# Two short segments' depthwise convolution on TensorE, and the scan's x multiplied from PSUM, in a Mamba-2 and gated-FFN kernel

## The chip, the cores and the metric

The kernel runs on one core of one Trainium2 chip. The metric is the device time of one launch in microseconds. The core has five engines that run side by side and wait for one another through semaphores: TensorE (PE, matrix products, into PSUM), VectorE (DVE), ScalarE (ACT), GpSimd (POOL, which works on SBUF alone here) and SyncE (SP, which issues most transfers). PSUM has eight banks of 512 fp32 columns here.

## The reference

The input is u of 4 batches x 1024 tokens x 256 features. One layer of two halves follows, each with a residual and layernorms (`_layernorm` without weights), all in fp32:

```
x = x + LN(mamba2(LN(x)))          # 4 x 1024 tokens, 256 features
x = x + LN(ffn(LN(x)))

mamba2(u):
  z, xBC, dt = split(u @ in_proj)            # 512, 768, 8 columns
  xBC = silu(b + sum_k w[:, k] * xBC[t - 3 + k])   # depthwise, causal, 4 taps
  x, B, C = split(xBC)                       # 512 (8 heads x 64), 128, 128
  dt = softplus(dt + dt_bias); dA = -exp(A_log) * dt
  y_t = C_t . S_t,  S_t = exp(dA_t) S_{t-1} + B_t (dt_t x_t);  y += D * x
  y = rmsnorm(y * silu(z)) * norm_weight;  return y @ out_proj

ffn(x): gate, up: 256 -> 2048 with 4-bit weights and a scale per 32; gelu(gate) * up;
        down: 2048 -> 256 with 4-bit weights and scales
```

## The kernel before

**Segments.** `SEGS` (line 25) cuts the 4096 tokens into nine segments: the first 512 tokens of batch 0 as two short segments, 0 and 1, of 256 tokens each, then seven of 512. A segment first goes through `mixer(s)` (line 646, the Mamba half) and then through `ffn(s)` (line 962). Features lie on partitions: the 768 columns of xBC are six tiles of 128 (`NF`), with tokens along the free axis.

**The mixer.** `norm_in` normalises and turns tokens around to `xnT`. `step_sizes` makes dt and dA, `decays` their running sums and exponentials. `features(f)` (line 753) multiplies one tile of in_proj by `xnT` into a PSUM bank `pp`, and forms the convolution: ScalarE writes `h`, tile f of `xc`, as `pp * w3 + b`; VectorE then adds the three earlier taps, one instruction each, from shifted views of `pp`. Weights and bias are halved once in `prepare_small` (line 558), so that `(tanh(h) + 1) * h` is the silu: ScalarE makes the tanh into `th`, VectorE the product. The last three columns of `pp` are saved in `tails[b]` for the next segment of the batch; `carried` (line 736) has GpSimd work out, from the tails of the segment before, the share of the first three columns (`edge`), which VectorE adds.

`inner(i)` (line 776) works on one block of 128 tokens: the decays between tokens (`e`), then four transposes of `xc` into a bank `px`, which ScalarE copies to `xt` (line 813), and from which VectorE makes `xdt` = x dt and `xw` = x dt decay (lines 816 and 819); GpSimd makes `y` = x D; two more products give C.B and B turned around. `gate(c)` makes silu(z), `scan(i)` the three products of the scan, `gated`, `way_out` and `turned` the gating, the output projection, the residual, and the turned input of the second half, `xfT`.

**The second half.** For segments 0 and 1 `widen(n)` makes gate and up of 128 hidden units in one bank (16 times), `narrow` the down product. Later segments use a scheme of seven products for eight blocks (`seven`), for which `weight_sums` forms sums of the weights on GpSimd in the tile `sums` and stores them by transfers (`stock`). `unpack` (line 585) turns 4-bit weights into fp32 in the opening: VectorE on the codes, GpSimd on the products with the scales (`wide`, `wd`).

**The order of work.** Nothing is issued as it is written. `Recorder` takes down every operation with its buffers; `issue` (line 260) then plans: at each step it takes, for each engine, the operations that could start soonest by its own table of costs (`weigh`, line 227) and picks by `rank`. Buffers come from pools and are assigned in that plan. The result is one fixed order per engine, and each engine runs its queue strictly in that order, so every instruction has line 347 in the profile and is told by its tiles. For VectorE instructions without a PSUM operand the plan adds up to `PORT` ns while GpSimd is at work, as long as the planned time is below `EARLY` (lines 33 and 311). The waiting room within which rank may prefer a later operation is 150 ns before `EARLY` and 30 ns after it (line 1135). Forty `WARM` products of the identity with itself (lines 1099 to 1104) have the last rank and fill TensorE in the opening.

**PSUM.** Two banks `a` serve the mixers, four `f` the gate and up products, two `d` the down products. The mixer of segment 0 takes its banks from `f`, that of segment 1 alternately from `d` and `a` (`ps_a`, line 654).

Of the kernel before, what the change touches and what calls it, by code (L numbers as in the profile page):

```python
# [24 lines left out]
SEGS = [(0, 0, 256), (0, 256, 256)] + [(b, 0, 512) for b in range(1, NB)] + \  # L25
    [(b, 512, 512) for b in range(NB)]
TMAX = 512
# [2 lines left out]
PORT = 700.0  # L30
SWITCH = 1400.0
WARM, WARM_FROM = 40, 9000.0
EARLY = 60000.0
FRONT = 2 + 1 + NF
MASKED = -1.0e30
MLP = 2048
# [337 lines left out]
def mamba_ffn_kernel(  # L374
# [19 lines left out]
    r = Recorder(tc.nc)  # L394
# [11 lines left out]
    def given(ap):  # L406
# [10 lines left out]
    pools = {  # L417
        "x": pool("x", [P, CMAX, DM], 3), "xnT": pool("xnT", [P, 2, TMAX]),
        "xc": pool("xc", [P, NF, TMAX]), "xn": pool("xn", [P, DM], 2, 3), "th": pool("th", [P, TMAX], 3, 3),
        "sz": pool("sz", [P, DI // P, TMAX]), "r": pool("r", [P, DI // P, P], 2), "e": pool("e", [P, NH, P], 2), "xt": pool("xt", [P, DI], 2),  # L420
        "bt": pool("bt", [P, DS], 2), "xdt": pool("xdt", [P, NH, HD], 2),
        "xw": pool("xw", [P, NH, HD], 2), "y": pool("y", [P, DI // P, P], 3),
        "yo": pool("yo", [P, DI // P, P]), "xf": pool("xf", [P, 2, P], 2),
        "xfT": pool("xfT", [P, 2, TMAX], 2), "act": pool("act", [P, HALF], 3, 3),
        "fo": pool("fo", [P, DM], 2), "cst": pool("cst", [CMAX * NH, P], 2),
        "rows": pool("rows", [CMAX * NH, P], 2, of=hbm), "dec": pool("dec", [P, 3 * CMAX * NH], 2),
        "edge": pool("edge", [P, NF, 3], 2), "part": pool("part", [P, NF, 3], 2),
        **{k + who: pool(k + who, shape, 4, 4) for who in "mf"
           for k, shape in (("mv", [P, CMAX, 2]), ("st", [P, 6]), ("rs", [P, CMAX]))},
        "one": pool("one", [P, 1], 24, 8),  # L430
# [4 lines left out]
    def get(tag):  # L435
        return pools[tag].get()
# [96 lines left out]
    def over_heads(v, n):  # L533

        return v.unsqueeze(2).to_broadcast([P, NH, n])
# [19 lines left out]
        return mv  # L555


    def prepare_small():

        r.scalar.activation(aneg, aneg, AF.Exp)  # L560
        r.vector.tensor_scalar_mul(aneg, aneg, -1.0)
        r.floor = 7500.0
        r.vector.tensor_scalar_mul(cw, cw, 0.5)
        r.vector.tensor_scalar_mul(cb, cb, 0.5)
        r.floor = 0.0

    def prepare_z():
# [76 lines left out]
    xfT = {}  # L644

    def mixer(s):
# [88 lines left out]

        def carried():
            v_["xc"] = by_segment(s, "xc", lambda t, c: t[:, :, c])
            if t0 == 0:
                return

            tail = tails[b]
            edge = v_["edge"] = get("edge")
            part = get("part")
            for k in range(3):
                n = 3 - k
                to = part if k else edge
                r.gpsimd.tensor_tensor(to[:, :, :n], tail[:, :, k:],
                                        cw[:, :, k : k + 1].to_broadcast([P, NF, n]), ALU.mult)
                if k:
                    r.gpsimd.tensor_tensor(edge[:, :, :n], edge[:, :, :n], part[:, :, :n],  # L750
                                            ALU.add)

        def features(f):

            xnT, xc = v_["xnT"], v_["xc"]
            pp = ps_a()
            for kk in range(2):
                r.tensor.matmul(pp[:, :T], lhsT=win[:, kk, DI + f * P : DI + (f + 1) * P],
                                 rhs=xnT[:, kk, :], start=(kk == 0), stop=(kk == 1))
            h = xc[:, f, :]  # L760
            r.scalar.activation(h, pp[:, :T], AF.Identity, scale=cw[:, f, 3:4],
                                 bias=cb[:, f : f + 1])
            if t0 + T < L:
                r.scalar.copy(tails[b][:, f, :], pp[:, T - 3 : T])
            if t0 > 0:
                r.vector.tensor_tensor(h[:, 0:3], h[:, 0:3], v_["edge"][:, f, :], ALU.add)
            for k in (2, 1, 0):
                d = 3 - k
                r.vector.scalar_tensor_tensor(h[:, d:T], pp[:, 0 : T - d], cw[:, f, k : k + 1],
                                               h[:, d:T], ALU.mult, ALU.add)  # L770
            th = get("th")[:, :T]
            r.scalar.activation(th, h, AF.Tanh)
            r.vector.scalar_tensor_tensor(h, th, 1.0, h, ALU.add, ALU.mult)


        def inner(i):
            if i == 0 and s + 1 < len(SEGS) and s + 1 not in xs:
                load_x(s + 1)
            xnT, xc = v_["xnT"], v_["xc"]
            tok = slice(i * P, (i + 1) * P)  # L780
            hs = slice(i * NH, (i + 1) * NH)
            last = t0 + T == L and i == NC - 1
            n = f"{s}_{i}"

            e_ = v_["e", i] = get("e")
            if s == 0:


                raw = []
                for h in range(NH):  # L790
                    if h % 4 == 0:
                        bank = banks_a.get()
                        for k in range(4):
                            r.tensor.matmul(bank[:, k * P : (k + 1) * P], lhsT=ident, rhs=masked,
                                            start=(k == 0), stop=False, skip_group_check=True)
                    raw.append(bank[:, h % 4 * P : (h % 4 + 1) * P])
                    j = i * NH + h
                    r.tensor.matmul(raw[h], lhsT=v_["da"][:, j : j + 1].to_broadcast([P, P]),
                                    rhs=upper, start=False, stop=True, skip_group_check=True)
            else:  # L800
                r.sync.dma_start(out=e_, in_=v_["rows"][hs, :].partition_broadcast(P))
                r.gpsimd.affine_select(out=e_, in_=e_, compare_op=ALU.is_ge, fill=MASKED, base=0,
                                        pattern=[[0, NH], [1, P]], channel_multiplier=-1)
                raw = [e_[:, h, :] for h in range(NH)]
            for h in range(NH):
                j = i * NH + h
                r.scalar.activation(e_[:, h, :], raw[h], AF.Exp, bias=v_["ncs"][:, j : j + 1])

            px = ps_a()
            for f in range(4):  # L810
                r.tensor.transpose(px[:, f * P : (f + 1) * P], xc[:, f, tok], ident)
            xt = get("xt")
            r.scalar.copy(xt, px)
            xt = xt.rearrange("p (h c) -> p h c", c=HD)
            xdt = v_["xdt", i] = get("xdt")
            r.vector.tensor_tensor(xdt, xt, over_heads(v_["dt"][:, hs], HD), ALU.mult)
            if not last:
                xw = v_["xw", i] = get("xw")
                r.vector.tensor_tensor(xw, xt, over_heads(v_["dtd"][:, hs], HD), ALU.mult)

            y = v_["y", i] = get("y")
            r.gpsimd.tensor_tensor(y, xc[:, 0:4, tok],
                                    dsk.unsqueeze(2).to_broadcast([P, DI // P, P]), ALU.mult)

            if t0 > 0 or i > 0:
                rr = v_["r", i] = get("r")
                if s == 0:
                    bank = banks_a.get()
                    for h in range(NH):
                        j = i * NH + h  # L830
                        r.tensor.matmul(bank[h % 2 * HD : (h % 2 + 1) * HD, h // 2 * P :][:, :P],
                                        lhsT=v_["da"][:, j : j + 1].to_broadcast([P, HD]),
                                        rhs=upper, start=True, stop=True)
# [286 lines left out]
    for s in range(ns):  # L1120
# [11 lines left out]
            r.floor = 0.0  # L1132
        if s + 2 < ns:
            do("mix", s + 2, mix[s + 2])
    r.issue(tc, rank, lambda e, at: 150.0 if at < EARLY else 30.0)


# [49 lines left out]
```

## Time and profile before

| | |
|---|---|
| median of 3 runs | 1052.22 us (1049.74 to 1054.22) |
| profiled execution | 1053.14 us |
| its span, first to last instruction | 1051.4 us |
| mean granted TensorE clock | 0.982 |
| TensorE, VectorE, ScalarE, GpSimd busy | 97%, 63%, 47%, 32% |
| first gate/up product of segment 0 | 67.0 us |
| first step-size product of segment 2 | 126.5 us |
| last matmul ends | 1042.8 us |

The profile is of one execution. Its times count from the first instruction. A group of instructions is written as engine, operation, output<-inputs by tile names (without buffer numbers), shape and count, then busy time and the mean duration of one; what follows the second bar is the idle time of the engine just before them, with what ended it. An fp32 matrix product appears as two records, a transpose as one. Matmul ends are modelled, so that neighbouring records can overlap in the busy time and a gap can be hidden in it.

### The profile page before, as it was taken

To read this page: it belongs to the slowest core of one execution; us is meant where nothing else is said; L and a number is where in the kernel's file an instruction comes from. 1 tells how busy PE (TensorE), PEld (TensorE's weight loads), DVE (VectorE), ACT (ScalarE), POOL (GpSimd) and SP (SyncE) were. 2 spreads that over 40 slices of the span, in tenths; PEclk is the share of its full clock that TensorE was granted. 3 is DMA by queue.
4 is the path that set the end of the run, shared out by engine and by line. 5 is a ranking of instruction groups with operands and counts; after the bars stand their busy time and mean duration, and the time that the engine had idled before them with its cause. 6 is when DMAs were issued, how large, how long until landed. Compare 5 with 4: busy or idle time off the path is not lost.

```text
span 1051.4 us, 14546 instructions
## 1 busy us (share of the span) xinstructions
PE 1016.3 (97%) x5174; PEld 815.6 (78%) x5174; DVE 665.2 (63%) x1443; ACT 498.3 (47%) x1146; POOL 336.3 (32%) x519
## 2 busy tenths in 40 slices
PE   8988899999999899999999999999999999999996
PEld 6676777887788677886688767887787778888885
DVE  5977786557666566658756766667666775434432
ACT  4536256625753365535673355547344752321330
POOL 1855735440234222413333044402550236001002
PEclk8989899999999999999999999999999999999998
DMA  6123151132321251132332133113222430232300
GB/s 217 33 49 141 41 181 70 52 126 94 132 91 38 78 156 59 63 141 71 106 125 71 70 101 131 71 70 131 71 96 75 132 116 30 76 122 99 147 4 20
DMA packets 39456, 97.16 MB, mean 92 GB/s; under 512 B 3800, under 2 KB 29896, under 8 KB 35272
## 3 DMA queue, kind: packets, MB, share of 16 engines
q1 hardware_dynamic: 38808, 96.22, 27.1%
q8 instruction: 40, 0.66, 0.3%
q14 instruction: 32, 0.26, 0.1%
q10 hardware_dynamic: 576, 0.02, 0.0%
HBM read 84.58 MB, written 11.66 MB: 92 GB/s over the span
## 4 chain that ended last, share of the span: by engine, by line
PE 87%; DVE 5%; POOL 4%; issue 1%; ACT 1%; DMA 1%; POOLq 0%; ACTq 0%; DVEq 0%
PE f L347 36%; PE a L347 29%; PE d L347 22%; DVE xc L347 1%; DVE wd L347 1%; POOL rsf L347 1%; POOL fo L347 1%; POOL y L347 1%; DVE fo L347 1%; DVE xw L347 1%; POOL wide L347 0%; POOL e L347 0%; DVE stf L347 0%; POOL state L347 0%; DMA aneg<-in_a_log_dram 0%
## 5 line engine op out<-in xcount | busy, mean ns | idle before, releaser
L347 PE MATMUL f<-wide 128*128 128x256 f32 x880 | 254.2, 384 | 4.4 <-DVE f L347 4.4
L347 PE MATMUL d<-wd,big 128*128 128x256 f32 x1024 | 254.2, 381 | 0.0
L347 PE MATMUL f<-xfT,wide 128*128 128x256 f32 (+1 forms) x1024 | 253.5, 361 | 0.5 <-ACT xfT L347 0.5
L347 PEld LDWEIGHTS d<-wd,big 128*128 128x128 f32 x1024 | 189.9, 190 | 32.2 <-issue 9.1
L347 PEld LDWEIGHTS f<-xfT,wide 128*128 128x128 f32 x1024 | 178.4, 197 | 32.2 <-issue 13.2
L347 PEld LDWEIGHTS f<-wide 128*128 128x128 f32 x880 | 160.8, 190 | 39.4 <-issue 13.8
L347 DVE TENSOR_TENSOR f<-f,sums 128x256 f32<-128x256 f32 x216 | 91.9, 429 | 91.9 <-PE f L347 88.4
L347 PE MATMUL a<-xnT,win 128*128 128x512 f32 (+1 forms) x300 | 140.4, 594 | 1.0 <-ACT xt L347 1.0
L347 DVE SCALAR_TENSOR_TENSOR xc<-a,cw,xc 128x511 f32<-128x511 f32 (+1 forms) x135 | 97.8, 725 | 7.7 <-ACT tail L347 5.7
L347 ACT ACTIVATE big<-f 128x512 f32<-128x512 f32 x108 | 62.7, 597 | 67.4 <-DVE f L347 38.0
L347 DVE TENSOR_TENSOR big<-big,f 128x512 f32<-128x512 f32 x108 | 72.8, 684 | 33.0 <-PE f L347 19.2
L347 ACT COPY f<-f 128x256 f32<-128x256 f32 x104 | 37.5, 360 | 109.8 <-PE f L347 99.8
L347 PEld LDWEIGHTS a<-xnT,win 128*128 128x128 f32 x300 | 55.1, 192 | 41.7 <-issue 35.3
L347 ACT ACTIVATE e<-e,ncs 128x128 f32<-128x128 f32 x240 | 73.8, 390 | 8.6 <-POOL e L347 8.5
L347 ACT ACT_TABLE_LOAD x58 | 74.4, 1283 | 3.8 <-issue 2.8
L347 POOL TENSOR_SCALAR rsf<-mvf 128x1 f32<-128x1 f32 x32 | 7.9, 246 | 197.0 <-DVE mvf L347 195.2
L347 POOL TENSOR_TENSOR state<-state,dec 128x512 f32<-128x512 f32 x24 | 25.8, 1077 | 129.1 <-PE a L347 122.9
L347 POOL TENSOR_TENSOR y<-xc,dsk 128x512 f32<-128x512 f32 x32 | 34.3, 1088 | 87.3 <-PE f L347 47.5
L347 ACT ACTIVATE xc<-a,cb,cw 128x512 f32<-128x512 f32 (+1 forms) x45 | 34.3, 763 | 57.6 <-PE a L347 57.5
L347 PE MATMUL a<-wo,y 128*128 128x256 f32 x232 | 55.4, 381 | 0.0
L347 POOL TENSOR_TENSOR sz<-sz 128x256 f32<-128x256 f32 x64 | 40.0, 626 | 41.0 <-ACT sz L347 39.8
L347 PEld LDWEIGHTS a<-wo,y 128*128 128x128 f32 x232 | 43.4, 190 | 6.4 <-DVE stm L347 0.5
(242 smaller groups left out, 1423.3 us busy)
## 6 DMA issues: line engine op xcount, KB each, us to landing
wide<-stock SPq DMA_DIRECT2D x28, 1792.0 KB, 7.4
e<-rows SPq DMA_DIRECT2D x30, 512.0 KB, 4.1
r<-rows SPq DMA_DIRECT2D x54, 128.0 KB, 4.4
stock<-sums SPq DMA_DIRECT2D x8, 512.0 KB, 2.6
out_dram<-fo SPq DMA_DIRECT2D x32, 128.0 KB, 1.7
x<-in_u_dram SPq DMA_DIRECT2D x7, 512.0 KB, 3.9
stock<-wide SPq DMA_DIRECT2D x6, 512.0 KB, 6.1
win<-in_w_in_dram SPq DMA_DIRECT2D x2, 512.0 KB, 6.6
```

The costliest lines, as they stand in the source:

```text
L347: getattr(getattr(self.nc, st.queue), st.name)(*[real(a) for a in st.args], **{k: real(a) for k, a in st.kwargs.items()})
```

## The change

Three things change.

In segments 0 and 1 the convolution becomes matrix products. `prepare_small` has GpSimd build, for each feature tile, four diagonal 128 x 128 matrices with the halved weights of the four taps. They lie in memory that is wanted only later: the scan states of batches 1 to 3 (`state[1..3]`), one of the two `xfT` buffers, and half of `sums`. In `features` ScalarE copies `pp` to a new SBUF tile `hp` with room for three columns in front, where for segment 1 the tails of segment 0 go. Four products with the diagonals, of shifted views of `hp`, accumulate in a second bank `pc`. ScalarE makes both tanh and `h` from `pc`, with the bias; the silu product on VectorE stays. `carried` does nothing more for segment 1.

In all segments `xt` is gone: `xdt` and `xw` are made by VectorE straight from the bank `px`, which is free once both are done.

`EARLY` goes from 60000 to 150000, with the waiting room of 150 ns still ending at 60000.

```diff
-EARLY = 60000.0
+EARLY = 150000.0
...
-        "xt": pool("xt", [P, DI], 2),
+        "hp": pool("hp", [P, 3 + SEGS[0][2]], 2),
...
+    rooms = [state[1], state[2], state[3], *(lambda v: (v[:, :DI], v[:, DI:]))(
+        get("xfT").rearrange("p k t -> p (k t)")),
+             sums.rearrange("p k c -> p (k c)")[:, :DI]]
+
+    def taps(f, k):
+        return rooms[(f + 2) % NF][:, k * P : (k + 1) * P]
...
         r.vector.tensor_scalar_mul(cw, cw, 0.5)
         r.vector.tensor_scalar_mul(cb, cb, 0.5)
+        for f in (4, 5, 0, 1, 2, 3):
+            r.gpsimd.tensor_tensor(rooms[(f + 2) % NF].rearrange("p (k c) -> p k c", k=4),
+                                   ident.unsqueeze(1).to_broadcast([P, 4, P]),
+                                   cw[:, f, :].unsqueeze(2).to_broadcast([P, 4, P]), ALU.mult)
...
-            if t0 == 0:
+            if t0 == 0 or s < 2:
                 return
...
             h = xc[:, f, :]
-            r.scalar.activation(h, pp[:, :T], AF.Identity, scale=cw[:, f, 3:4],
-                                 bias=cb[:, f : f + 1])
+            th = get("th")[:, :T]
+            if s < 2:
+                hp = get("hp")
+                if t0 > 0:
+                    r.scalar.copy(hp[:, 0:3], tails[b][:, f, :])
+                r.scalar.copy(hp[:, 3:], pp[:, :T])
             if t0 + T < L:
                 r.scalar.copy(tails[b][:, f, :], pp[:, T - 3 : T])
-            if t0 > 0:
-                r.vector.tensor_tensor(h[:, 0:3], h[:, 0:3], v_["edge"][:, f, :], ALU.add)
-            for k in (2, 1, 0):
-                d = 3 - k
-                r.vector.scalar_tensor_tensor(h[:, d:T], pp[:, 0 : T - d], cw[:, f, k : k + 1],
-                                               h[:, d:T], ALU.mult, ALU.add)
-            th = get("th")[:, :T]
-            r.scalar.activation(th, h, AF.Tanh)
+            if s < 2:
+                pc = ps_a()
+                for k in (3, 2, 1, 0):
+                    d = 0 if t0 > 0 else 3 - k
+                    r.tensor.matmul(pc[:, d:T], lhsT=taps(f, k), rhs=hp[:, k + d : k + T],
+                                     start=(k == 3), stop=(k == 0), skip_group_check=True)
+                r.scalar.activation(th, pc[:, :T], AF.Tanh, bias=cb[:, f : f + 1])
+                r.scalar.activation(h, pc[:, :T], AF.Identity, bias=cb[:, f : f + 1])
+            else:
...
             r.vector.scalar_tensor_tensor(h, th, 1.0, h, ALU.add, ALU.mult)
...
-            xt = get("xt")
-            r.scalar.copy(xt, px)
-            xt = xt.rearrange("p (h c) -> p h c", c=HD)
+            px = px.rearrange("p (h c) -> p h c", c=HD)
             xdt = v_["xdt", i] = get("xdt")
-            r.vector.tensor_tensor(xdt, xt, over_heads(v_["dt"][:, hs], HD), ALU.mult)
+            r.vector.tensor_tensor(xdt, px, over_heads(v_["dt"][:, hs], HD), ALU.mult)
             if not last:
                 xw = v_["xw", i] = get("xw")
-                r.vector.tensor_tensor(xw, xt, over_heads(v_["dtd"][:, hs], HD), ALU.mult)
+                r.vector.tensor_tensor(xw, px, over_heads(v_["dtd"][:, hs], HD), ALU.mult)
...
-    r.issue(tc, rank, lambda e, at: 150.0 if at < EARLY else 30.0)
+    r.issue(tc, rank, lambda e, at: 150.0 if at < 60000.0 else 30.0)
```

The branch under the last `else` of `features` holds the old instructions, unchanged, for segments 2 to 8.

More of the change, by code (lines that the diff above doesn't have):

```diff
@@ L419, in mamba_ffn_kernel @@
         "xc": pool("xc", [P, NF, TMAX]), "xn": pool("xn", [P, DM], 2, 3), "th": pool("th", [P, TMAX], 3, 3),
-        "sz": pool("sz", [P, DI // P, TMAX]), "r": pool("r", [P, DI // P, P], 2), "e": pool("e", [P, NH, P], 2), "xt": pool("xt", [P, DI], 2),
+        "sz": pool("sz", [P, DI // P, TMAX]), "r": pool("r", [P, DI // P, P], 2), "e": pool("e", [P, NH, P], 2),
         "bt": pool("bt", [P, DS], 2), "xdt": pool("xdt", [P, NH, HD], 2),
@@ L426, in mamba_ffn_kernel @@
         "rows": pool("rows", [CMAX * NH, P], 2, of=hbm), "dec": pool("dec", [P, 3 * CMAX * NH], 2),
-        "edge": pool("edge", [P, NF, 3], 2), "part": pool("part", [P, NF, 3], 2),
+        "hp": pool("hp", [P, 3 + SEGS[0][2]], 2), "edge": pool("edge", [P, NF, 3], 2), "part": pool("part", [P, NF, 3], 2),
         **{k + who: pool(k + who, shape, 4, 4) for who in "mf"
@@ L760, in features @@
             h = xc[:, f, :]
-            r.scalar.activation(h, pp[:, :T], AF.Identity, scale=cw[:, f, 3:4],
-                                 bias=cb[:, f : f + 1])
+            th = get("th")[:, :T]
[4 more added lines that the diff above has]
+                r.scalar.copy(hp[:, 3:], pp[:, :T])
             if t0 + T < L:
                 r.scalar.copy(tails[b][:, f, :], pp[:, T - 3 : T])
-            if t0 > 0:
-                r.vector.tensor_tensor(h[:, 0:3], h[:, 0:3], v_["edge"][:, f, :], ALU.add)
-            for k in (2, 1, 0):
-                d = 3 - k
-                r.vector.scalar_tensor_tensor(h[:, d:T], pp[:, 0 : T - d], cw[:, f, k : k + 1],
-                                               h[:, d:T], ALU.mult, ALU.add)
-            th = get("th")[:, :T]
-            r.scalar.activation(th, h, AF.Tanh)
+            if s < 2:
[7 more added lines that the diff above has]
+            else:
+                r.scalar.activation(h, pp[:, :T], AF.Identity, scale=cw[:, f, 3:4],
+                                     bias=cb[:, f : f + 1])
+                if t0 > 0:
+                    r.vector.tensor_tensor(h[:, 0:3], h[:, 0:3], v_["edge"][:, f, :], ALU.add)
+                for k in (2, 1, 0):
+                    d = 3 - k
+                    r.vector.scalar_tensor_tensor(h[:, d:T], pp[:, 0 : T - d],
+                                                   cw[:, f, k : k + 1], h[:, d:T],
+                                                   ALU.mult, ALU.add)
+                r.scalar.activation(th, h, AF.Tanh)
             r.vector.scalar_tensor_tensor(h, th, 1.0, h, ALU.add, ALU.mult)
```

## The prediction

> **What bounds the kernel now.** I read the page's busy shares and slices first, then the stretches as a table, then TensorE's forms in the opening, then the two multiplies that the change touches.
>
> ```profile
> PE 1016.3 (97%) x5174; PEld 815.6 (78%) x5174; DVE 665.2 (63%) x1443; ACT 498.3 (47%) x1146; POOL 336.3 (32%) x519
> ...
> PEclk8989899999999999999999999999999999999998
> ```
>
> TensorE is busy for 97% of the span; a reader is tempted to stop here and charge every added matmul in full. The busy time by stretch says where that would be wrong (per engine: us busy and instructions, then granted clock, DMA share, GB/s):
>
> ```profile
> 0.00:8.80 8.80, 3.78 (x16) 3.49 (x16) 1.62 (x7) 1.49 (x2) 3.83 (x19) 1.00 0.68 197
> 8.80:67.00 58.20, 54.26 (x318) 41.36 (x318) 46.72 (x99) 31.61 (x83) 35.37 (x42) 0.93 0.39 105
> 67.00:130.00 63.00, 55.21 (x363) 49.09 (x364) 47.86 (x107) 26.03 (x68) 35.28 (x48) 0.88 0.21 76
> 130.00:1051.40 921.40, 903.05 (x4479) 721.66 (x4477) 569.03 (x1233) 439.14 (x993) 261.79 (x412) 0.99 0.27 92
> ```
>
> After 130 us TensorE runs at one record per slot: in the chain of work ten records of 256 columns take 2.16 us, 0.216 each (an fp32 matmul is two records). Before 130 us the same engine has fewer records than time, though "busy" hides it, because modelled ends cover the gaps and a slowed clock. So I count the opening by form (records; us busy, mean ns; idle before):
>
> ```profile
> L347 PE MATMUL f<-xfT,wide 128*128 128x128 f32 x202 | 30.6, 310 | 0.5 <-ACT xfT L347 0.5
> L347 PE MATMUL f<-xnT,win 128*128 128x256 f32 x40 | 12.8, 462 | 0.0
> L347 PE MATMUL f<-ident 128*128 128x128 f32 x80 | 10.8, 280 | 0.0
> L347 PE MATMUL d<-wide,spread 8*128 8x512 f32 x16 | 8.4, 626 | 0.0
> ```
>
> All rows of that view, by start-to-start distances in the timeline: 112 records of 256 columns x 0.216 = 24.2; 202 gate/up records of 128 x 0.111 = 22.4; 194 others of up to 128 columns x 0.111 = 21.5; 16 scale products x 0.52 = 8.3; 13 of 512 x 0.43 = 5.6; 80 half-width ones x 0.055 = 4.4. Sum 86.4 us of work. The 80 `f<-ident` records are the 40 fillers (8.9 us). So 34.7 of the first 130 us are waiting or half clock: 7.0 before 8.8 us (loads, first norm) and 27.7 after. The clock shares, 0.93 of 58.2 us and 0.88 of 63, mean 8.1 + 15.1 us at half rate, at most 11.6 of the 27.7. There VectorE sets the pace: busy 46.7 of 58.2 us, stretched by sharing with GpSimd:
>
> ```profile
> L347 DVE TENSOR_TENSOR xdt<-xt,dt x32: 657/693/1581, 36.5 to 866.1; 128x512 f32<-128x512 f32 x32
> L347 ACT COPY xt<-a x30: 563/586/605, 85.3 to 864.8; 128x512 f32<-128x512 f32 x30
> ```
>
> ```profile
> 36.45 1.58 DVE L347 TENSOR_TENSOR xdt<-xt,dt 128x512 f32<-128x512 f32 x1
> 37.96 1.59 DVE L347 TENSOR_TENSOR xw<-xt,dtd 128x512 f32<-128x512 f32 x1
> ```
>
> (ns: least, median, most; then two of them in order of time.) 693 ns at rest, 1.58 us while GpSimd's eight `wide` products run (34.7 to 45.8).
>
> **What the Trainium skill says.** "TensorE: Matmul & The Clock Gate", Part 1, What's actually happening: the clock is halved after about 3.4 us without activity and given back after about as long busy. The trace agrees: after a 3.38 us gap at 364 us, four records of 512 columns take 3.56 us instead of 1.88. "GPSIMD Engine Reference", Specifications: GpSimd and VectorE contend when the latter has two SBUF inputs; the 1.58 against 0.69 above agrees. "VectorE: DVE Perf Modes", The perf-mode tier table: fp32 `tensor_tensor` runs at one element per cycle from SBUF or PSUM, so a PSUM source is no slower; `y<-a,y`, 685 ns from PSUM, agrees.
>
> **The change part by part.**
>
> 1. *TensorE gains.* Two segments x six feature tiles x four products of 253 to 256 columns = 48 matmuls, 96 records x 0.216 = 20.7 us. Nothing on TensorE goes. If nothing hid it: +20.7.
>
> 2. *VectorE loses, all before 130 us.* 36 tap instructions of 475 to 481 ns (17.2 us) and six edge adds (1.5). The eight early `xdt`/`xw` take 1.40 us on average; from PSUM I take 0.69 (the row `yo<-f,r`): 5.7 less. Together 24 of the 94.6 us in 8.8:130.
>
> 3. *ScalarE.* 12 copies `hp` (256 columns, as `xnT<-f`, 375 ns) are 4.5 us, six 3-column ones 0.9; four `xt` copies (2.4) go. Net +3, on an engine busy 57.6 of 121 us: hidden unless a copy is late, when the taps behind it on TensorE's queue are late.
>
> 4. *GpSimd.* Six diagonal products of 512, like `y<-xc,dsk` (1.09 to 1.18): 6.5 to 7 us. They stand right behind the first `rsm`, where GpSimd is idle from 11.4 to 28 us; the first is done near 10.4 (scaled weights at 9.2, plus 1.1), before the first copy of features can start (12.3). Cost nothing; without that cover, 1.1 us per tile. The second pair of `rsm` slips behind them to about 16.8: it serves segment 1's tokens, wanted much later. Segment 1's five edge operations (1.1 us) go. The diagonal for tile 3 lies in `sums`, so the first of the 32 weight sums, which stands ahead of segment 1's `y` and mask on GpSimd, waits for the last tap product: `y` needs that tile anyway, the mask and the exponentials perhaps 3 us later. On SP the three `stock<-wide` transfers now stand ahead of segment 1's `e` and `r` rows: 2.5 us of issue (the trace's 81.97 to 84.50) and their bytes; both delays overlap.
>
> 5. *All segments.* 28 more `xt` copies go (16 us of ScalarE, beside work). The other 52 multiplies lose only their contention: 60 at a mean of 0.89 is 53.4, less 41 at 0.69, less the 5.7 above, about 6 us, off the path. But the bank is now held until both multiplies are done (0.2 + 2 x 0.69, 1.6 us) instead of one copy (0.8). In the built order the next product into that bank stands 2.2 us of TensorE work behind (median; 1.3 before), so the margin stays about half a microsecond.
>
> 6. *The planner's constant.* EARLY keeps the port penalty in the plan to 150 us. It changes order alone: before segment 2's step sizes 27 more gate/up matmuls (6.0 us) and five more down ones (2.2) are placed.
>
> **The sum.** Up to the first gate/up product the changed order holds 46.1 us of work (counted as above) and 36 fillers (8.0): no earlier than 8.8 + 54.1 = 62.9, against 67.0 now. Following the queues by hand with the rows' durations, VectorE's `xf` there falls at about 60 (GpSimd's last `one` and `rsm` near 59.5), so fillers cover it; TensorE finds its operands there 0.5 to 1 us ahead nearly everywhere. I put 1.5 us of waits to that point and 3.5 from there to segment 2 (the second `xf`, the later exponentials). Then the opening is 20.7 - 27.7 + 5.0 = -2.0. Break-even is 7.0 us of waits. Later than 130 us, 18.3 us are idle, 8.6 of them the tail after the last matmul. Two waits there end on the copy that goes:
>
> ```profile
> 499.78 3.70 PE L347 MATMUL a<-xnT,win 128*128 128x512 f32 x8 [0.35 <-ACT xt L347]
> ```
>
> With the one at 628 they sit in stretches of 15 us with 1.7 and 1.8 us idle, the second also at half clock (0.89, 1.7 us): 5.2 in all; I take 3, with 0 and -8 as ends. Total -5 us. The profiled execution took 1053.1 us (span 1051.4, 1.7 outside), 0.9 above the median of 1052.2: 1048.1 there, **1047** for the median.
>
> **Rivals.**
> *The opening closes up* (likeliest): waits 2 to 6 us, later gain 2 to 7: 1040 to 1049 us. For: VectorE loses a quarter of its opening, every added product falls where TensorE was short of work.
> *It cancels:* waits near 7 to 10, later gain 0 to 3: 1048 to 1056. For: 20.7 and 27.7 are near each other, and half-clock stretches need only one long gap each.
> *ScalarE feeds the taps late, slower:* each of 12 tap groups waits for an `hp` copy queued in order behind 1.9 us byte copies (`wd<-big`), `wo` passes and table loads of 1.28. TensorE waits in order, so everything behind waits too. At 1 us per group, +12: 1047 + 12 = 1059. It decides from 0.9 us per group (1047 + 10.5 is 0.5% above before), from 0.6 with the later gain gone. Against: most gaps are 0.5 to 1 us in hand, and gate/up work stands between the groups of segment 1.
> *The bank is held too long, slower:* if half of the 28 later blocks overrun their 2.2 us by 1 us, 14 us more: 1061. Against: VectorE has no contention there any more.
>
> **Numbers.** Closing up 0.46, cancelling 0.28, ScalarE late 0.18, bank held 0.08. Less than 0.5% (5.3 us) is about what a measurement of this kernel can tell from no change: faster 0.46, within 0.28, slower 0.26. The likeliest one's own range is 1040 to 1049; 8 in 10 need 1038 to 1061 (waits of 0 to 17 us, later gain 8 to 0).
>
> **What would show it.** First gate/up product at 63 to 65 us; fillers partly in front of it; clock above 0.95 in 8.8:67 and 67:130; `xdt` and `xw` near 0.69 us throughout; segment 2's first step-size product at about 132 (126.5 now). Wrong: taps with waits on `hp` above 0.8 us each, `a` products waiting on `xw`, or exponentials later than 98 us with all four `f` banks full.

## The result, and the profile after

The changed kernel takes 1056.99 us in the median of 6 runs (1054.90 to 1059.96), the kernel before, on the same chip, 1049.86 (6 runs, 1048.25 to 1054.22). The ratio is 1.0064, with a 95% interval of 1.0038 to 1.0089: slower by 0.6%. The prediction had 1047, from a kernel before that stood at 1052.22 in the three runs known then.

The profiled execution of after took 1056.95 us with a span of 1055.2, 3.8 us more than the span of before. The medians differ by 7.1, because the profiled execution of before (1053.14) lay 3.3 us above its median. The traces can therefore explain 3.8 us; the rest is spread between executions.

The page of after, busy shares and granted clock by slice:

```profile
PE 1030.6 (98%) x5270; PEld 829.3 (79%) x5270; DVE 637.1 (60%) x1401; ACT 479.2 (45%) x1126; POOL 330.2 (31%) x520
...
PEclk9999999998999999999999999999999999999998
```

The 96 added TensorE records are there (5270 against 5174), VectorE has lost 28 us and the clock row has lost its eights in the opening. All three say what the change meant to do. The same stretches as before (per engine: us busy and instructions, then clock, DMA share, GB/s):

```profile
0.00:8.80 8.80, 3.78 (x16) 3.48 (x16) 1.36 (x6) 1.49 (x2) 3.81 (x19) 1.00 0.68 184
8.80:67.00 58.20, 57.92 (x308) 45.41 (x309) 30.23 (x72) 30.13 (x81) 32.02 (x39) 0.97 0.32 100
67.00:130.00 63.00, 61.06 (x444) 55.44 (x443) 35.15 (x82) 28.34 (x81) 34.64 (x45) 1.00 0.26 82
130.00:1055.20 925.20, 907.88 (x4507) 724.99 (x4505) 570.39 (x1244) 419.24 (x963) 259.70 (x419) 0.99 0.27 91
```

TensorE looks full up to 67 us, yet it has only 308 records there, fewer than the 318 of before, although 48 of them are tap products. "Busy" covers half clock and fillers. TensorE's forms in the first 130 us:

```profile
L347 PE MATMUL f<-xfT,wide 128*128 128x128 f32 x207 | 26.2, 277 | 0.4 <-ACT xfT L347 0.4
L347 PE MATMUL f<-xnT,win 128*128 128x256 f32 x40 | 11.8, 434 | 0.0
L347 PE MATMUL f<-ident 128*128 128x128 f32 x80 | 11.3, 301 | 0.0
...
L347 PE MATMUL d<-wide,spread 8*128 8x512 f32 x16 | 8.4, 626 | 0.0
...
L347 PE MATMUL d<-hp,state 128*128 128x256 f32 x24 | 5.5, 378 | 0.0
```

I counted both traces again in one way: each record is given the median start-to-start distance of its shape, fillers apart, and what is left, from the first product at 3.0 us on, is waiting or half clock.

| us | before | after | difference |
|---|---|---|---|
| TensorE work | 952.0 | 972.9 | +20.9 |
| waiting and half clock, 3.0 to 8.8 us | 4.0 | 4.3 | +0.3 |
| the same, 8.8 to 130 us | 30.9 | 14.0 | -16.9 |
| the same, 130 to 260 us | 4.6 | 13.3 | +8.7 |
| the same, 260 us to the last matmul | 39.0 | 30.0 | -9.0 |

(The prediction's count by rounded rows gave 27.7 for the 30.9, and its 7.0 ahead of 8.8 us begins with the span.) Other groupings of the shapes give 14 to 16 us for the 16.9 and leave the last two differences within 0.4 us. The sum, +4.0, is the span's +3.8 within rounding. The opening hid 16.9 of 20.9 us. What was won after 260 us came back as a lump of waits before 260. Where that lump sits, by TensorE in order of time:

```profile
237.14 0.44 PE L347 MATMUL a<-ident,xf 128*128 128x128 f32 x2
238.04 0.51 PE L347 MATMUL a<-ident,xn 128*128 128x128 f32 x2 [0.46 <-ACT xfT L347]
241.22 0.69 PE L347 MATMUL a<-ident,xf 128*128 128x128 f32 x2 [2.67 <-DVE xf L347]
...
242.85 2.05 PE L347 MATMUL f<-wide 128*128 128x256 f32 x4
244.70 1.06 PE L347 MATMUL a<-ident,xn 128*128 128x128 f32 x4
```

TensorE waits for the last turned block of segment 2 and has no gate, up or down product of segments 0 and 1 left to put in front. Part of the lump is half clock: the four records from 242.85 us take 0.46 us each where 0.22 is the rate, and the trace's clock records grant half from 240.1 to 246.9 us, which by the rates of its records costs some 2.5 us. In before no half clock lies between 130 and 260 us. The same block on VectorE, after and then before:

```profile
240.75 0.41 DVE L347 TENSOR_SCALAR xf<-x,mvm,rsm 128x256 f32<-128x256 f32 x1 [0.95 <-POOL rsm L347]
```

```profile
226.61 0.41 DVE L347 TENSOR_SCALAR xf<-x,mvm,rsm 128x256 f32<-128x256 f32 x1 [0.95 <-POOL rsm L347]
```

It is 14.1 us later. From this block to the end of the span are 814.4 us in after and 824.8 in before, which still had 20 records (4.3 us) of down products to do there and waited 9.0 us longer after 260. So there are two questions for the experiments: what moves this block, the fourth `xf` of segment 2, and to which part of the change the shorter rest belongs.

The operands of the scan do what was forecast (ns: least, median, most):

```profile
L347 DVE TENSOR_TENSOR xdt<-a,dt x30: 678/691/692, 98.3 to 864.9; 128x512 f32<-128x512 f32 x30
...
L347 DVE TENSOR_TENSOR xdt<-f,dt x2: 692/692/692, 41.6 to 44.9; 128x512 f32<-128x512 f32 x2
```

And the list of TensorE's waits by releaser (us in total, times, longest) clears two rivals: no wait ends on `hp`, and one of 0.7 us ends on `xw`.

```profile
PE a L347 <- DVE xf L347: 2.7, 1, 2.7
...
PE a L347 <- DVE xw L347: 0.7, 1, 0.7
```

Now the place where the first gate/up product was expected at 63 to 65 us. TensorE, VectorE and GpSimd in order of time:

```profile
63.40 0.38 PE L347 MATMUL f<-ones,sz 128*128 128x1 f32 x2
...
63.90 5.08 PE L347 MATMUL f<-ident 128*128 128x128 f32 x44
68.81 0.38 PE L347 MATMUL f<-ident,xf 128*128 128x128 f32 x2
69.03 1.73 PE L347 MATMUL f<-ident 128*128 128x128 f32 x14
70.59 1.95 PE L347 MATMUL f<-xfT,wide 128*128 128x128 f32 x16
```

```profile
62.61 0.48 DVE L347 SCALAR_TENSOR_TENSOR x<-f,one,x 128x256 f32<-128x256 f32 x1 [3.83 <-POOL one L347]
...
66.72 0.41 DVE L347 TENSOR_SCALAR xf<-x,mvm,rsm 128x256 f32<-128x256 f32 x1 [1.88 <-POOL rsm L347]
...
69.57 1.31 DVE L347 TENSOR_SCALAR xn<-x,mvm,rsm 128x256 f32<-128x256 f32 x1
```

```profile
49.89 2.16 POOL L347 TENSOR_TENSOR wide<-wd,big 128x512 f32<-128x512 fp8e4 x2 [7.54 <-ACT big L347]
...
62.01 0.56 POOL L347 TENSOR_TENSOR one<-one,mhalf 128x1 f32<-128x1 f32 x1
62.54 3.22 POOL L347 TENSOR_TENSOR wide<-wd,big 128x512 f32<-128x512 fp8e4 x3
65.85 0.19 POOL L347 TENSOR_SCALAR rsm<-mvm 128x1 f32<-128x1 f32 x1
```

From 63.9 to 70.6 us TensorE runs fillers and two transposes. `xf`, forecast at about 60, comes at 66.72, because GpSimd makes three unpacking products between the `one` and the `rsm` that it needs: `mvm`, the input of `rsm`, was done at 63.77 and had to wait until 65.85. When `xf` is there, at 67.1, some fifteen records of fillers still stand ahead of its transposes, 1.7 us.

### The profile page after: what moved, and what is told of

Same layout as the page of the kernel before. It is cut to its first block, busy times and chain, and to the rows that moved or that the text cites. A ratio compares the mean times of both kernels' runs of the same rounds, so it can differ in the third digit from the quotient of the medians.

```text
span 1055.2 us, 14695 instructions
## 1 busy us (share of the span) xinstructions
PE 1030.6 (98%) x5270; PEld 829.3 (79%) x5270; DVE 637.1 (60%) x1401; ACT 479.2 (45%) x1126; POOL 330.2 (31%) x520
## 5 line engine op out<-in xcount | busy, mean ns | idle before, releaser
L347 PE MATMUL f<-xfT,wide 128*128 128x256 f32 (+1 forms) x1024 | 250.2, 355 | 0.9 <-ACT big L347 0.5
L347 PEld LDWEIGHTS f<-xfT,wide 128*128 128x128 f32 x1024 | 172.7, 191 | 27.3 <-issue 7.8
L347 DVE SCALAR_TENSOR_TENSOR xc<-a,cw,xc 128x511 f32<-128x511 f32 (+2 forms) x126 | 93.7, 745 | 11.6 <-ACT xc L347 9.3
L347 ACT ACTIVATE big<-f 128x512 f32<-128x512 f32 x108 | 63.0, 597 | 75.6 <-DVE f L347 48.3
L347 POOL TENSOR_SCALAR_AFFINE_SELECT e<-e 128x1024 f32<-128x1024 f32 x30 | 33.3, 1113 | 75.8 <-DMA e<-rows 75.6
L347 PEld LDWEIGHTS a<-wo,y 128*128 128x128 f32 x232 | 43.3, 190 | 8.1 <-DVE x L347 1.5
L347 ACT ACTIVATE xc<-a,cb,cw 128x512 f32<-128x512 f32 x42 | 32.8, 780 | 33.7 <-PE a L347 33.7
```

The lines of the kernel that those rows point to most:

```text
L347: getattr(getattr(self.nc, st.queue), st.name)(*[real(a) for a in st.args], **{k: real(a) for k, a in st.kwargs.items()})
```

## The experiments

Eighteen kernels, in groups of two or four, each group beside runs of the kernel before on the same chip. Kernels are compared by the difference of their ratios, turned into microseconds at 1051 us, about what before takes. Such a difference is uncertain by about 0.3%, 3 us. The columns on the right are of the profiled execution: segment 1's first step-size product, segment 2's fourth `xf`, and the time from it to the end of the span. In e8 and e16 that execution lay 3.7 and 4.8 us above the median.

| kernel | median us | ratio to before, 95% | seg. 1 from | 4th `xf` | rest |
|---|---|---|---|---|---|
| before | | | 57.1 | 226.6 | 824.8 |
| after, the whole change | 1056.99 | 1.0064 (1.0038 to 1.0089) | 75.7 | 240.8 | 814.4 |
| e1 px alone | 1045.65 | 0.9938 (0.9924 to 0.9951) | 57.9 | 229.6 | 814.8 |
| e2 EARLY alone | 1049.55 | 0.9983 (0.9969 to 0.9997) | 62.1 | 226.3 | 824.7 |
| e3 products alone | 1053.37 | 1.0024 (1.0009 to 1.0038) | 62.1 | 234.8 | 817.5 |
| e4 products and px | 1058.80 | 1.0053 (1.0032 to 1.0073) | 76.0 | 244.0 | 813.4 |
| e5 after, scale products first | 1050.03 | 0.9992 (0.9968 to 1.0015) | 63.1 | 235.3 | 813.6 |
| e6 after, products for segment 1 only | 1047.78 | 0.9966 (0.9950 to 0.9982) | 57.5 | 230.4 | 813.5 |
| e7 after, products for segment 0 only | 1057.23 | 1.0068 (1.0042 to 1.0094) | 74.0 | 238.9 | 814.0 |
| e8 after, 8 fillers | 1052.75 | 1.0028 (1.0014 to 1.0042) | 74.0 | 239.6 | 815.2 |
| e9 px, scale products held to 44 us | 1038.93 | 0.9876 (0.9859 to 0.9892) | 67.3 | 222.5 | 814.8 |
| e10 px, scale products first | 1046.84 | 0.9954 (0.9939 to 0.9969) | 63.0 | 229.8 | 815.2 |
| e11 e6, scale products first | 1050.56 | 0.9991 (0.9981 to 1.0001) | 66.4 | 234.8 | 813.4 |
| e12 e5, 8 fillers | 1053.27 | 1.0013 (0.9997 to 1.0028) | 65.2 | 239.4 | 813.8 |
| e13 after, gate/up of segment 1 narrowed | 1054.11 | 1.0036 (1.0023 to 1.0050) | 75.6 | 237.5 | 814.6 |
| e14 e6, scale products held to 44 us | 1049.43 | 0.9988 (0.9970 to 1.0007) | 67.2 | 235.5 | 813.9 |
| e15 after, scale products held to 44 us | 1058.83 | 1.0079 (1.0052 to 1.0106) | 83.3 | 245.7 | 813.8 |
| e16 after, taps narrowed | 1051.09 | 1.0007 (0.9992 to 1.0022) | 77.9 | 239.2 | 814.9 |
| e17 before, scale products held to 44 us | 1049.58 | 0.9990 (0.9976 to 1.0003) | 67.3 | 236.9 | 813.9 |
| e18 px, scale products held to 40 us | 1047.25 | 0.9959 (0.9944 to 0.9974) | 67.3 | 228.3 | 816.2 |

The last column is the steadiest thing in this study: in all kernels with the px part it is 813.4 to 816.2 us, whatever the opening did. The time of each is decided before segment 2's fourth `xf`.

**Which part.** Three theories went into the first four runs: A, the added records cost what the opening cannot absorb; B, the bank px is held too long; C, the planner's constant EARLY spoils the order.

e1, before with this edit:

```diff
-            xt = get("xt")
-            r.scalar.copy(xt, px)
-            xt = xt.rearrange("p (h c) -> p h c", c=HD)
+            px = px.rearrange("p (h c) -> p h c", c=HD)
...
-            r.vector.tensor_tensor(xdt, xt, over_heads(v_["dt"][:, hs], HD), ALU.mult)
+            r.vector.tensor_tensor(xdt, px, over_heads(v_["dt"][:, hs], HD), ALU.mult)
```

> The kernel before, with one part of the change: xdt and xw made straight from the bank px in all segments, no xt. Convolution on VectorE and EARLY = 60000 as before. Theory A (the 96 added records on TensorE cost what the opening cannot absorb): 1045 to 1050 us, no slower than before. Theory B (the bank px is held too long): slower than before by about what the whole change is, 1056 us. Theory C (the planner's constant and the new order): 1048 to 1050.

e2, before with `EARLY = 150000.0` and the waiting room still ending at 60000:

```diff
-EARLY = 60000.0
+EARLY = 150000.0
...
-    r.issue(tc, rank, lambda e, at: 150.0 if at < EARLY else 30.0)
+    r.issue(tc, rank, lambda e, at: 150.0 if at < 60000.0 else 30.0)
```

> The kernel before, with EARLY = 150000 alone (the waiting room still ends at 60000); nothing else is changed. Theory A and theory B: within 3 us of before, 1047 to 1053. Theory C (the order from the planner's constant costs the time): 1055 or more.

e3, after with `xt` back (one buffer) and EARLY at 60000:

```diff
-EARLY = 150000.0
+EARLY = 60000.0
...
+            xt = get("xt")
+            r.scalar.copy(xt, px)
+            xt = xt.rearrange("p (h c) -> p h c", c=HD)
```

> The changed kernel with xt kept (one buffer of it instead of two, for room) and EARLY = 60000: of the change only the convolution of segments 0 and 1 as products. Theory A: slower than before, 1053 to 1060, with a segment 2 step-size product near 137 us or later. Theory B and theory C: 1047 to 1051.

e4, after with this alone:

```diff
-EARLY = 150000.0
+EARLY = 60000.0
```

> The changed kernel with EARLY = 60000: convolution and px parts, without the planner's constant. Theory A: 1053 to 1058, like the whole change. Theory B: 1055 to 1058. Theory C: 1047 to 1051, and then the constant is what cost the time.

Measured: e1 0.9938, e2 0.9983, e3 1.0024, e4 1.0053. B falls: the px part alone gains 0.6%. C falls: the constant alone gains a little, and without it the rest is as slow as the whole. A is left: the products are what costs. (Even A missed in one place: e3's first step-size product of segment 2, expected near 137 us or later, came at 119.1.) And the parts do not add up. -0.62, -0.17 and +0.24% make -0.55%, and the whole is +0.64%. With the px part in place the products cost 12 us (e4 against e1), without it 2.5 (e3 against before, with the caveat of its single `xt` buffer).

**Which segment, and is it the order?** In after, six of eight `d<-wide,spread` products stand at 48 to 63 us; before had all of them done by 42.4. GpSimd, idle from 32 to 50 us but for two `y`, then makes twelve unpacking products between the steps of the norms (the GpSimd lines above). From this I formed theory D: segment 0's tap products push the scale products back, and that is what makes everything late.

e5, after with

```diff
+                key, r.key = r.key, ("scale", 0)
                 r.tensor.matmul(bank, lhsT=spread, rhs=few[:, cols], start=True, stop=True)
...
+                r.key = key
...
-            "warm": 1000, "wu": 11, "x": 5}[kind]
+            "warm": 1000, "wu": 11, "x": 5, "scale": 9}[kind]
```

> The changed kernel with one rank altered: the eight scale products d<-wide,spread of the first two weight tensors, and the copies big<-d that read them, get rank 9, ahead of the mixer of segment 0 (10). Nothing is left out. Theory D (the tap products of segment 0 push six of the eight scale products to 48 to 63 us; GpSimd is idle from 32 to 50 us and then has twelve wide products to make among the steps that the first turned block xf and segment 1's norm wait for): 1046 to 1050 us, first gate/up product by 66 us, segment 1's first step-size product by 66. Theory A (the added work itself): 1054 to 1058, the products only trade places.

e6 and e7, after with the products for one segment alone:

```diff
-            if t0 == 0 or s < 2:
+            if t0 == 0 or s == 1:
...
-            if s < 2:
+            if s == 1:
```

> The changed kernel with the convolution of segment 0 back on VectorE; only segment 1's is made of products (48 records of the 96). The scale products stand early again in this order. Theory D: 1044 to 1049, as fast as the px part alone or faster, since nothing is pushed. Theory A (each added record costs): half of the loss against the px part alone, about 1051.

```diff
-            if t0 == 0 or s < 2:
+            if t0 == 0:
...
-            if s < 2:
+            if s == 0:
```

> The changed kernel with the convolution of segment 1 back on VectorE, with its edges on GpSimd; only segment 0's is made of products. The scale products stand as late as in the changed kernel. Theory D: 1055 to 1058, the whole loss or more. Theory A: about 1051, as with segment 1 alone.

e8, after with

```diff
-WARM, WARM_FROM = 40, 9000.0
+WARM, WARM_FROM = 8, 9000.0
```

> The changed kernel with 8 fillers instead of 40; nothing of the result is left out. If the fillers that stand ahead of xf (44 records from 63.9 us, 14 from 69.0, 8 from 72.4) cost time, up to 3.6 us are given back: 1053 to 1054. If the clock then halves in the hole that they filled, 1057 or more. Theories A and D say no more of it than that its loss lies elsewhere.

Measured: e5 0.9992, 7.6 us better than after; e6 0.9966; e7 1.0068, the whole loss; e8 1.0028, 3.8 us better. The times of e5, e6 and e7 came out as D expected. A, which had 1054 to 1058 for e5 and about 1051 for the other two, missed all three. The 3.8 us of e8 are about what the trace said of fillers ahead of ready work, though its interval just overlaps that of after. One expectation of D failed: e5's first gate/up product is at 83.4 us and not by 66, though segment 1 starts at 63.1. With the times alone, D would have been the answer. But all of these runs change the products and the order together, so D still had to stand by itself: late scale products in a kernel with no tap product on TensorE.

**D alone.** e9, e1 with

```diff
+                if room is big[0] or q > 1:
+                    r.floor = 44000.0
                 r.tensor.matmul(bank, lhsT=spread, rhs=few[:, cols], start=True, stop=True)
+                r.floor = 0.0
```

> The px part alone (as e1, no product of the convolution on TensorE), with six of the eight early scale products held back in the plan to 44 us, so that they stand as late on TensorE as in the changed kernel, with GpSimd's wide products behind them. No work is added to e1 and none left out. Theory D (lateness of the scale products, and of segment 1's norm behind them): 1051 to 1054, segment 1's first step-size product near 70 us, segment 2's last turned block xf some 6 us later than e1's 229.6 us. Theory A (only added records cost): 1045 to 1047, as e1.

e10, e1 with the edit of e5; e11, e6 with the edit of e5; e12, e5 with the edit of e8:

> The px part alone (as e1), with the eight scale products at rank 9. In e1 they stand early by themselves, so theory D and theory A both expect 1043 to 1047; a gain would say that the before order, too, has them too late.

> As e6 (products for segment 1's convolution alone) with the scale products at rank 9. Theory D: 1044 to 1048, as e6, whose scale products are early already. The time from segment 2's last turned block xf to the end is expected at 814 us, as in the six kernels with the px part so far (813.4 to 815.2).

> As e5 (the whole change with the scale products at rank 9) with 8 fillers instead of 40. If what fillers cost (3.8 us between the changed kernel and e8) adds to what the rank gave (7 us): 1045 to 1048. If e5 has few fillers on its path, as its 2.7 us of them between 67 and 130 us say: 1048 to 1050.

Measured: e9 0.9876, that is 1038.9 us, the fastest kernel of the study and 6.5 us faster than e1, where D had it slower by as much. D falls, and A, which had e9 no faster than e1, did not foresee it either. The scale products do stand late in e9 (six of them at 50 to 61 us) and segment 1 starts at 67.3, but GpSimd's queue fell into another order (e9, GpSimd and then VectorE in order of time):

```profile
50.45 0.56 POOL L347 TENSOR_TENSOR one<-one,mhalf 128x1 f32<-128x1 f32 x1
52.04 2.16 POOL L347 TENSOR_TENSOR wide<-wd,big 128x512 f32<-128x512 fp8e4 x2 [1.04 <-ACT big L347]
54.16 1.26 POOL L347 TENSOR_TENSOR sz<-sz 128x256 f32<-128x256 f32 x2
55.50 0.19 POOL L347 TENSOR_SCALAR rsm<-mvm 128x1 f32<-128x1 f32 x1
```

```profile
56.38 1.18 DVE L347 TENSOR_SCALAR xf<-x,mvm,rsm 128x256 f32<-128x256 f32 x1 [2.79 <-POOL rsm L347]
```

The scale products had let segment 0 pass, and its first `xf` came at 56.4 us against 65.5 in e1. e10 is as fast as e1, as both theories had it. Nor do the other edits add: e11, expected at 1044 to 1048, is if anything slower than e6 (0.9991 against 0.9966, intervals just touching), and e12, with fewer fillers and expected at 1050 at most, no faster than e5 (1.0013 against 0.9992), where after gained 3.8 us from the same edit.

**Work or order.** Left were W, that TensorE's own work up to the fourth `xf` counts, and S, that the serial chain of the mixers and norms counts and TensorE's records only fill it. Two runs keep the order of every queue as in after and only shorten records; the plan is told the old cost. e16 narrows three of four tap products to 32 columns, and so leaves out the earlier taps of most tokens:

```diff
-                    r.tensor.matmul(pc[:, d:T], lhsT=taps(f, k), rhs=hp[:, k + d : k + T],
+                    e = T if k == 3 else d + 32
+                    st = r.tensor.matmul(pc[:, d:e], lhsT=taps(f, k), rhs=hp[:, k + d : k + e],
...
+                    st.busy = 2 * (T - d) * 0.837
```

> The changed kernel with the order of every queue unchanged, but three of the four tap products of each tile on 32 columns instead of 253 to 256 (they leave out the earlier taps of most tokens): 72 records shorter by 0.15 to 0.19 us, 11 to 13 us less TensorE work before 130 us. Theory W (TensorE's work in the opening is on the path): 1045 to 1049. Theory S (a serial chain over the other engines): 1053 to 1057.

e13 narrows segment 1's gate and up products of the second half of the features to 32 columns too, and so leaves that half out for most tokens:

```diff
+                        k = 32 if s == 1 and kk else step
-                        r.tensor.matmul(bank[:, m * T + i * step : m * T + (i + 1) * step],
+                        st = r.tensor.matmul(bank[:, m * T + i * step : m * T + i * step + k],
...
-                                        rhs=xfT[s][:, kk, i * step : (i + 1) * step],
+                                        rhs=xfT[s][:, kk, i * step : i * step + k],
...
+                        st.busy = 2 * max(109.0, step * 0.837)
```

> The changed kernel with the order of every queue unchanged, but segment 1's gate and up products of the second half of the features on 32 columns instead of 256 (that half is left out for most tokens): 64 records shorter by 0.15 to 0.19 us, 10 to 12 us less TensorE work, all between 80 us and the lump of waits at 228 to 247 us. Theory W: 1045 to 1047, the whole of it. Theory S (segment 2's mixer is what is late at 228 us, TensorE only waits longer there): 1053 to 1057.

e14 is e6, and e15 is after, each with the edit of e9:

> As e6 (products for segment 1's convolution alone) with six scale products held back to 44 us in the plan as in e9. If the order of e9 is what made it fast and segment 1's products cost little (e6 against e1: 2 us): 1038 to 1042. If they collide there: 1046 or more. The time from segment 2's last turned block to the end: 814 us, as in the eleven kernels with the px part.

> The whole change with six scale products held back to 44 us in the plan as in e9. Against e9 (1038.9) it adds the tap products alone: 20.7 us of records. If the products cost what they cost against e1 (11 us): 1050. If that order can absorb nothing: 1057 to 1060. If the change only lacked e9's order: 1039 to 1043.

Measured: e16 1.0007, 6.0 us less than after, for 8.4 us of work taken out (972.9 to 964.6; the narrow records saved less than I had put). The intervals of e16 and after do not touch. e13 1.0036, 2.9 us less for 9.3 us taken out (963.6), and its interval overlaps that of after. So in the opening work counts, for some 6 of 8 us, and later for little or nothing: neither W nor S alone. e16's own trace shows where some of it goes (TensorE in order of time):

```profile
63.68 7.52 PE L347 MATMUL f<-ident 128*128 128x128 f32 x44
71.04 0.38 PE L347 MATMUL f<-ident,xf 128*128 128x128 f32 x2
```

Segment 0's mixer was ready earlier (`xf` at 64.3), but the same 44 fillers stood in front, and in that execution they ran at half clock: 7.5 us instead of 5.1.

e15, the whole change in the hold of e9, is 21.3 us slower than e9; e14, segment 1's products alone, 11.8 us slower. So the same 96 records cost 4.0 us where the scale products have rank 9 (e5 against e10), 12.1 in the order of the plan itself (e4 against e1) and 21.3 under the hold (e15 against e9). (The first and last pairs also differ in EARLY, which alone moved 1.8 us.)

**How much is order alone.** e17 puts e9's hold into the kernel before, e18 moves the hold in e9 to 40 us:

> The kernel before with six scale products held back to 44 us in the plan, as in e9, and nothing else changed (xt stays). If e9's gain over e1 (6.7 us) is the order's own: 1043 to 1046. If it needs the px part: 1049 to 1053.

> As e9, but held to 40 us in the plan instead of 44. If the gain belongs to late scale products as such: 1037 to 1041. If it belongs to the one order that e9's plan fell into: anywhere from 1040 to 1050. Time from segment 2's last turned block to the end again 813 to 815 us.

Measured: e17 0.9990, e18 0.9959. The gain of e9 is neither the hold's own nor that of late scale products: 4 us of planned hold shift the time by 8.7 us, with the same instructions. e9 is one lucky order, faster than both kernels of this case, and kept as such. e17 also answers the second question: with `xt` kept and no product of the convolution it has 813.9 us after the fourth `xf`. The shorter rest belongs to no part of the change. In e17, too, waiting and half clock go from after 260 us (39.0 to 28.7) to 130 to 260 us (4.6 to 16.4). Why they trade places so evenly was not tried.

## Why the prediction was wrong

**TensorE gains: right.** 20.7 us forecast, 20.9 counted, 96 records.

**VectorE loses: right in kind.** 24 us forecast in 8.8 to 130 us, 29.2 measured (94.6 to 65.4); `xdt` near 0.69 us in all 32, now from PSUM. The Trainium skill's "VectorE: DVE Perf Modes", The perf-mode tier table, has fp32 `tensor_tensor` in the same mode from SBUF and from PSUM, and this agrees.

**ScalarE: hidden, as forecast.** 57.6 to 58.5 us busy there, and no TensorE wait on `hp`. That rival falls.

**GpSimd.** The six diagonals (9.5 to 15.6 us) were free and the second `rsm` slipped to 15.9 (16.8 forecast). The part failed further on: I had GpSimd's last `one` and `rsm` near 59.5, and followed VectorE's `xf` to 60. The unpacking products interleaved with them put `rsm` at 65.85 and `xf` at 66.72, 6.7 us late.

**All segments.** The bank rival falls (one wait of 0.7 us, e1 faster). But the later gain of 3 us did not come either: after 130 us waiting and half clock are 43.6 in before and 43.3 in after. The waits after 260 us that I had hoped to see shrink did, by 9.0, and 8.7 came back as the lump at 228 to 247 us. This holds for e1 too (its 130 us onward: 43.6). What px gains there, it gains in the opening: 7.1 us less waiting by 130 us.

**The planner's constant.** By itself 0.2% faster, and no more than the forecast change of order.

**The sum: the step that failed.** "I put 1.5 us of waits to that point and 3.5 from there to segment 2." Measured: 9.3 and 4.7, so 14.0 for the 5.0. The first gate/up product came at 70.6 us, segment 2's first step-size product at 138.9 (132 forecast). Break-even was 7.0, so the sign turns in this term. Of the 9.3 us, 6.1 are half clock, which I had set to nothing. TensorE in order of time, after:

```profile
9.99 1.91 PE L347 MATMUL f<-ident 128*128 128x128 f32 x8
...
13.26 3.76 PE L347 MATMUL f<-xnT,win 128*128 128x256 f32 x8
```

The eight records from 9.99 us start 0.21 us apart, where the rate is 0.11 (the same eight took 0.89 us in before); the rate rises only at 18.1 us, and falls once more from 25.1 to 28.5. The Trainium skill says in "TensorE: Matmul & The Clock Gate", Part 1, What's actually happening, that the activity window runs freely, so that the cold time differs from run to run of one kernel. The traces agree: after ran at half rate from 9.1 to 18.1 us, e16, whose queues hold the same records in the same order up to there, from 10.8 to 17.6. A plan to erase all half clock by filling gaps was more than could be had: the stretch from 25.1 us has no gap ahead of it, but four records of scale products (the last section has more on this). My check "clock above 0.95" was met, 0.97 and 1.00, and did not show it: the trace's first clock record lies at 18.2 us, and the mean takes what is ahead of it as full.

The sum with measured terms, in the prediction's own count: -5.0, +7.8 and +1.2 for the two waits, +2.7 for the later gain (0.3 instead of 3), +0.3 for the first 8.8 us, -3.2 for what the prediction's count of before left out: +3.8, the difference of the spans.

**The rivals.** "It cancels", waits of 7 to 10 us with later gain near nothing, came nearest in mechanism; the waits were 14.0, and the measured 1057.0 lies 1 us above its 1048 to 1056. The two rivals on the slower side, which would have given 1059 and 1061, came near in time with mechanisms that the traces rule out.

**What stays open.** Shown: the loss comes with segment 0's products (e7), lies before segment 2's fourth `xf`, and follows TensorE's work in the opening when the order is held (6.0 of 8.4 us, e16), with perhaps 3.8 us of fillers in it (e8, at the edge of the noise). Not shown: one wait or step that carries the rest. The same records cost 4 to 21 us in three orders, and a theory that named one step of the order (D) passed by the times of three runs and fell in the first that tested it alone.

## What to carry to other kernels

When a list scheduler plans all engines anew, an edit's price includes the order that the new plan falls into; here a 4 us shift of one hold moved the time by 8.7 us with no instruction changed, more than the edit under study. Price an edit with the order held (shorten the instructions, tell the plan the old cost), and try a theory about the order in a kernel without the edit before believing it. Where an engine that is short of work is to absorb new work, do not count all its waits and half clock as room: of 30.9 us, 14.0 stayed, and fillers planned for a gap run in full even when the work behind them is ready.

## What the runs showed of the hardware that was not expected

The half rate also comes in stretches of 3.4, 6.8, 10.2 and 13.7 us within TensorE's continuous work. In e9 eight fillers took 0.11 us each from 9.8 to 10.7 us, and those from 15.9 to 17.5 us 0.21, with no gap between. A gap of 2.5 us had ended at 9.2, so the slow stretch came after the work had begun again, not in the gap. One execution of e16 had 13.7 us of it at 55 to 69 us, where after, with the same order, had none.

Many of these stretches follow the scale products (`d<-wide,spread`), whose weights fill 8 of the 128 rows. The 20 traces record 43 stretches that begin between 9 and 80 us. In 16 of them a gap of 1.2 to 3.1 us lies within the 3.4 us ahead or at the start. Before each of the other 27, scale products took 1.6 to 3.0 of the 3.4 us ahead; of all such windows from 17 to 66 us only 17% hold that much. Not every cluster is followed by one (that of after at 57 to 60 us is not), and no run changed these products alone, so the cause is not shown. Nor does it rank the kernels: e9, the fastest, has 10.2 us of half rate behind them.

Half clock is part of why single executions of one kernel spread over 2 to 12 us here: in each of the thirteen changed kernels with ten or more executions, those with the lower mean granted clock tended to take longer (correlations of -0.55 to -0.87). Nothing here says that it makes the whole change slower: the median granted clock of after is 0.990, that of before 0.987 in every group, though both means take what lies ahead of a trace's first clock record as full. Because of this spread the medians and intervals, not the traces, carry the verdicts above.
